# A two-layer graph network on one core: the order of work in the first hundred microseconds

## The chip, the cores and the metric

The kernel runs on one core of a Trainium2 chip, in one launch. The metric is the device time of that core in microseconds (us). Five instruction streams run side by side: TensorE (PE, with its weight loads PEld), VectorE (DVE), ScalarE (ACT), GpSimd (POOL) and SyncE (SP), which issues all the DMAs. Each stream executes its instructions in the order in which they were laid down[...].

## The reference

There are 64 graphs of 256 nodes with 512 features, and one adjacency matrix `adj` (256x256). Everything is float32.

```python
h = jnp.maximum(_layernorm(x, axis=-1), 0.0)
x = x + _L0_gnn_ref(h, adj, L0_gnn_W, L0_gnn_a)
h = jnp.maximum(_layernorm(x, axis=-1), 0.0)
x = x + _L1_gnn_ref(h, adj, L1_gnn_Wq, ...)
```

Layer 0 is a graph attention: `h = X @ W` (512 to 256 columns), two score columns `h @ a`, a leaky ReLU of their sum, the mask, a softmax, and `alpha @ h`; its result has 256 columns of `alpha @ h` and 256 of `h`. Layer 1 is an attention with 8 heads of 64: products of the normalized rows with Wq, Wk and Wv plus their biases, scores masked by `adj`, a softmax, the values weighed, and a product with Wo plus `bo`.

## The kernel before

**Groups and stages.** Two graphs form a group `g` of 512 rows (four tiles of 128), so there are 32 groups. `first_norm(g)` loads nothing itself: it measures the rows (`stats`), makes the normalized tiles `xn` on ACT, turns them, and puts them into `hT0`, the operand of layer 0. For group 0 the turning is done by transposes on PE (`pt`), for later groups by a round through memory: DVE transposes blocks into `xt`, SP sends `xt` to DRAM (`passed`) and fetches it back in another order (`moved`, four DMAs), and ACT copies it into the operand. `first_layer(g)` is layer 0: products `ph`, the tile `H`, the attention weights `e`, the products `po`, and then the second normalization into `hT1`, the operand of `project(g)`. `scores`, `weigh` and `outputs` are the attention and the last product (`sc`, `pr`, `py`).

For group 0 and 1, `first_layer` makes `ph` per row tile; the score row of group 1 goes from `H` by a DVE transpose (`rows`) to DRAM (`line`) and comes back spread over all partitions (`own`); then ACT makes `e` from it, DVE takes the leaky ReLU, ACT the exponential, and DVE multiplies it by `maskT`.

**Seven products.** The products with Wq, Wk, Wv, Wo and, from group 2 on, W are done by a scheme that multiplies two by two blocks with seven products in place of eight. Each product of `project` is four matmuls of 128x256. Products 1 and 2 use raw blocks of operand and weights. Product 6, 5, 7 and 3 need sums of operand blocks (`operand_sums`, four POOL instructions that write `sums` and a block of `hT`), and 3, 4, 5, 6, 7 need sums of weight blocks (`weight_sums`, four subtractions in place). Products 1, 6, 5 and 3 build up in one held bank of PSUM, and between them ACT takes copies (`kept`) out of it; 7 and 4 build up in a second one; product 2 uses one of the five turning banks of `mm`.

**The judge.** The kernel's fast path leaves out the subtraction of the row maximum. `judge()` shows that the inputs allow that: two products of each of Wq and Wk with itself (`gram`), squared twice (`square_q`, `square_k`, with ACT copies `room` between), and several sums of squares. `mask()` also tests that every row has an edge and that `adj` holds only 0 and 1 (`bad`).

**The bias of the values.** `last_bias()` multiplies the rows of Wo by `bv` (`bv_rows`, four DVE instructions), sums them on PE (`pb`) and adds the sum to `b_out`, which `residual` adds to `x` on POOL.

**The order.** The engines' order is written out by hand. `not_sooner` and `in_order` tie an instruction to the one issued last on its engine; all matmuls and transposes are in the order of the program. The prologue (lines 1135 to 1163) advances generators letter by letter: `n` is a piece of `first_norm`, `0` and `1` pieces of `first_layer` of groups 0 and 1, `u` a product of `project(0)`, `c` a piece of the judge, `e` a piece of the mask, `s` again a piece of group 1. From line 1165 the loop over groups does the same with the strings in `steps`. SP's stream holds, in this order: the first loads and weights, `passed` and `moved` for the first half of group 1, and then `late_loads` (line 235), which are the two loads of group 2, eight DMAs of Wo, eight of `bv` and one of `bo`; only behind these come `passed` and `moved` of the second half of group 1, then `line` and `own`.

The prologue's lines in the kernel before:

```python
take(*"en00nn0e00n0cnn")
late_loads()
take(*"000n0c00n0n")
weight_sums("q")
take(*"euun0011")
order = "- nss n nn ns - s - ss ss s s n - n - s - s".split()
```

Of the kernel before, what the change touches and what calls it, by code (L numbers as in the profile page):

```python
# [57 lines left out]
def bounded(  # L58
# [87 lines left out]

    def warm_up():
        warm = mm("warm")
        for _ in range(12):
            matmul(warm[:, :P], square_ones, square_ones, start=True, stop=True)  # L150

    def load(g, b):
# [35 lines left out]
    def mask():  # L188
        edge = att.tile([P, NT, N], F32, tag="kept", name="edge", bufs=3)
        not_sooner(vector, "tensor_scalar", edge, adj_i, 0.0, None, op0=ALU.not_equal)  # L190
        yield
        pt = mm("pt_mask").rearrange("p (k q) -> p k q", k=NT)
        for kb in range(NT):
            for t in range(NT):
                transpose(
                    pt[:, kb, t * P : (t + 1) * P], edge[:, t, kb * P : (kb + 1) * P], ident
                )
        not_sooner(vector, "tensor_copy", maskT, pt)
        yield

        not_sooner(vector, "reduce_max", bad[:, 0, :], edge, axis=AX.X)
        vector.tensor_scalar(bad[:, 0, :], bad[:, 0, :], 0.0, None, op0=ALU.is_equal)
        vector.tensor_tensor(edge, edge, adj_i, op=ALU.not_equal)
        vector.reduce_max(bad[:, 1, :], edge, axis=AX.X)
        yield


# [22 lines left out]
    for name, src in (("q", bq), ("k", bk)):  # L230
        bcol[name] = const.tile([P, HP], F32, name=f"b{name}_sb")
        nc.sync.dma_start(bcol[name], src.rearrange("(c p) -> p c", p=P))
    load_weights("v", wvT)

    def late_loads():
        load(2, 0)
        load(2, 1)
        rows = woT.rearrange("(q j h d) o -> j h d q o", j=QH, h=2, d=S)
        bv_rows = bv.rearrange("(q j h d) -> j h d q", j=QH, h=2, d=S)
# [5 lines left out]
        for j in range(QH):  # L245
            for half in range(2):
                not_sooner(
                    sync, "dma_start", bv_col[j * S : (j + 1) * S, half, :], bv_rows[j, half]
                )
        not_sooner(  # L250
            sync, "dma_start", b_out,
            bass.AP(tensor=bo.tensor, offset=bo.offset, ap=[[0, P], [1, D]]),
        )

    rexp = const.tile([P, NT], F32, name="rexp")
    gpsimd.memset(rexp, -0.5)
# [9 lines left out]
    def first_weight_sums():  # L266
# [6 lines left out]
        not_sooner(gpsimd, "tensor_sub", t2, w22, w12)  # L273
        not_sooner(gpsimd, "tensor_sub", t4, w21, t2)

    def last_bias():


        rows = big.tile([P, 2, D // 2], F32, tag="oT0", name="bv_rows", bufs=1)
        for q in range(NQ):  # L280
            for half in range(2):
                of, by = w_sb["o"][:, half, 2 * q : 2 * q + 2, :], bv_col[:, half, q : q + 1]
                if q == half == 0:
                    not_sooner(vector, "tensor_scalar", rows, of, by, None, op0=ALU.mult)
                else:
                    vector.scalar_tensor_tensor(rows, of, by, rows, op0=ALU.mult, op1=ALU.add)
        yield
        pb = mm("pb")
        matmul(pb, square_ones, rows.rearrange("p o n -> p (o n)"), start=True, stop=True)
        yield  # L290
        not_sooner(vector, "tensor_add", b_out, pb, b_out)
        yield
# [133 lines left out]
            vector.bn_stats(st, src[t])  # L426
        vector.bn_aggr(mv[:, t, :], st)

    put_last, norm_last, edge_last, sums_last = [], [], [], []

    def norm_T(src, mv, name, by_pe):

# [46 lines left out]
        def turn(b):  # L479
# [10 lines left out]
            for t in tiles:  # L490
                not_sooner(
                    vector, "transpose",
                    xt[:, :, :, t % NT, :], xn[t].rearrange("p (c j a) -> p j c a", j=J, a=S),
                )
            rows = passed[b], xt.rearrange("p j c t n -> p j (c t n)")
            if name[:2] == "0_" and name not in ("0_0", "0_1"):
                not_sooner(sync, "dma_start", *rows)
# [347 lines left out]

    def project(g):
        ops = operands.pop(g)
        for name in ("q", "k", "v"):
            shape = [P, NT, D] if name == "v" else [P, HP, N]
            turn[0] = 1 - turn[0]  # L850

            def blocks(bank):
                return bank.rearrange("p (o n) -> p o n", o=2)

            def product(out, i, start):
                a, w = ops[i][0], w_sb[name][:, :, ops[i][1], :]
                for o in range(2):
                    cols = slice(o * P, (o + 1) * P)
                    for c in range(2):
                        of, by = (a[:, c, cols], w[:, c, :]) if name == "v" else (w[:, c, cols], a[:, c, :])  # L860
                        matmul(
                            out[:, o, :], of, by, start=start and o == c == 0, stop=o == c == 1,
                            skip_group_check=True,
                        )

            def part(b, half):
                if (name, g, b) not in qkv:
                    qkv[name, g, b] = place(shape, f"{name}_{g}_{b}")
                to = qkv[name, g, b][0]
                if name == "v":  # L870
                    return to[:, :, half * D // 2 : (half + 1) * D // 2]
                return to[:, 2 * half : 2 * half + 2, :]

            def take(to, bank, half):

                behind = [scalar.last] if g == 0 and name != "v" else []
                if name == "v":
                    taken = [scalar.copy(to, bank)]
                else:
                    taken = [  # L880
                        scalar.activation(
                            to[:, o, :], bank[:, o, :], AF.Identity,
                            bias=bcol[name][:, 2 * half + o : 2 * half + o + 1], scale=1.0,
                        )
                        for o in range(2)
                    ]
                for last in behind:
                    for instruction in taken:
                        after(instruction, last)

            def kept(bank, half, i):
                s = att.tile([P, 2, N], F32, tag="kept", name=f"kept{i}_{name}_{g}", bufs=3)
                take(s, bank, half)
                return s

            first = blocks(held_bank(turn[0], f"p{name}1_{g}"))
            product(first, 1, True)
            p1 = kept(first, 0, 0)
            yield
            second = blocks(mm(f"p{name}2_{g}"))  # L900
            product(second, 2, True)
            vector.tensor_add(part(0, 0), second, p1)
            yield
            product(first, 6, False)
            p16 = kept(first, 0, 1)
            yield
            second = blocks(held_bank(1 - turn[0], f"p{name}7_{g}"))
            product(second, 7, True)
            p7 = kept(second, 1, 2)
            yield  # L910
            product(first, 5, False)
            vector.tensor_add(part(1, 1), first, p7)
            yield
            product(second, 4, False)
            vector.tensor_add(part(1, 0), second, p16)
            yield
            product(first, 3, False)
            take(part(0, 1), first, 1)
            yield

    def value_differences(g, b):

# [205 lines left out]
    def take(*names):  # L1128
        for name in names:
            next(work[name])  # L1130
# [461 lines left out]
```

## Time and profile before

| | us |
|---|---|
| median of 3 runs | 2413.16 (2413.15 to 2413.9) |
| the profiled execution: device time | 2416.09 |
| the profiled execution: span of the trace | 2414.4 |
| PE busy | 2387.8 |
| DVE busy | 1697.8 |
| POOL busy | 1422.3 |
| ACT busy | 1021.7 |

The profiled execution is 2.9 us longer than the median of the others, and 1.7 us of it lie outside its span. Matmul busy time covers 99% of the span, and the chain of work that ended last runs over PE for 96% of it. The 26.6 us in which no matmul ran lie almost wholly in the first 110 us and in the last 40. In lines of the timeline an entry gives start, duration, engine, source line, operation, output and inputs, and how often; a bracket gives idle time before it and what ended it. "SPq" lines are DMA issues on SP.

### The profile page before, as it was taken

What the parts mean: (1) busy time and instruction counts of PE and PEld (TensorE: products, weight loads), DVE (VectorE), ACT (ScalarE), POOL (GpSimd) and SP (SyncE); (2) the same over time, 40 slices, a digit from 0 to 9 for tenths busy, and PEclk for the clock granted to TensorE, in tenths of its full rate; (3) what the DMA queues carried; (4) which work ended last, traced back from release to release, by engine and by line L of the source; (5) the groups of instructions that cost most, each with busy time, mean ns of one, the idle gap of its engine ahead of it and who ended that gap; (6) DMA issues with size and microseconds to landing.
All of it is one profiled execution on the core that took longest, in us unless ns stands there. A gap on an engine that the chain in (4) does not pass through costs nothing.

```text
span 2414.4 us, 43064 instructions
## 1 busy us (share of the span) xinstructions
PE 2387.8 (99%) x15812; PEld 2012.6 (83%) x15812; DVE 1697.8 (70%) x3346; ACT 1021.7 (42%) x2017; POOL 1422.3 (59%) x1290
## 2 busy tenths in 40 slices
PE   7999999999999999999999999999999999999998
PEld 6788888888888888888888888888888888888886
DVE  6677767777667767667776667676677676676666
ACT  4444444444434444434444444444344344343431
POOL 3466666566566556565655666565655565656552
PEclk9999999999999999999999999999999999999999
DMA  5244444444455444544444544444554445554331
GB/s 179 92 142 143 139 155 149 144 153 139 142 159 160 144 136 140 157 148 154 152 136 139 161 149 145 145 143 145 153 166 145 136 136 162 149 159 141 111 103 44
DMA packets 272041, 343.76 MB, mean 142 GB/s; under 512 B 25424, under 2 KB 217168, under 8 KB 271824
## 3 DMA queue, kind: packets, MB, share of 16 engines
q1 hardware_dynamic: 271824, 340.95, 45.7%
q8 instruction: 126, 2.06, 0.4%
q14 instruction: 91, 0.75, 0.1%
HBM read 177.22 MB, written 163.64 MB: 141 GB/s over the span
## 4 chain that ended last, share of the span: by engine, by line
PE 96%; DVE 2%; DMA 1%; ACT 1%; issue 0%; SPq 0%; POOL 0%; DVEq 0%; ACTq 0%
PE pk L137 16%; PE py L137 16%; PE pv L137 16%; PE pq L137 16%; PE sc L137 10%; PE pr L137 9%; PE ph L137 8%; PE po L137 4%; DMA passed<-xt 0%; DVE st L35 0%; DVE x L35 0%; DMA wo_sb<-in_L_gnn_Wo_dram 0%; ACT e L35 0%; PE total L137 0%; DVE xt L35 0%
## 5 line engine op out<-in xcount | busy, mean ns | idle before, releaser
L35 POOL TENSOR_TENSOR p<-p 128x512 f32<-128x512 f32 x248 | 384.4, 1562 | 484.0 <-DVE p L35 466.6
L35 ACT ACTIVATE xn<-x,factor 128x512 f32<-128x512 f32 x256 | 194.8, 807 | 343.9 <-POOL factor L35 338.4
L35 DVE TENSOR_TENSOR p<-p,maskT 128x1024 f32<-128x1024 f32 x254 | 334.0, 1335 | 1.9 <-ACT p L35 1.9
L35 ACT ACTIVATE p<-sc 128x512 f32<-128x512 f32 x512 | 257.7, 624 | 138.0 <-PE sc L137 120.2
L35 DVE TENSOR_TENSOR x<-py,x 128x256 f32<-128x256 f32 x448 | 185.7, 415 | 184.4 <-PE py L137 178.1
L35 POOL TENSOR_TENSOR parts<-parts 128x512 f32<-128x512 f32 x248 | 248.1, 1000 | 83.5 <-DMA parts<-rows 61.2
L137 PE MATMUL py<-wo_sb,oT 128*128 128x256 f32 x1024 | 262.4, 379 | 0.6 <-DVE oT L35 0.6
L137 PE MATMUL sc<-q,k 64*128 64x256 f32 x2048 | 252.3, 390 | 0.3 <-ACT p L35 0.3
L137 PEld LDWEIGHTS sc<-q,k 64*128 64x128 f32 x2048 | 204.5, 186 | 48.6 <-issue 25.9
L137 PE MATMUL pk<-hT,wk_sb 128*128 128x256 f32 x1024 | 244.8, 382 | 0.0
L137 PE MATMUL pq<-hT,wq_sb 128*128 128x256 f32 x1024 | 240.1, 382 | 1.0 <-ACT hT L35 0.7
L137 PE MATMUL pv<-wv_sb,hT 128*128 128x256 f32 x1024 | 236.8, 379 | 0.0
L137 PE MATMUL pr<-p,v 128*32 128x256 f32 x4096 | 234.2, 380 | 0.0
L137 PEld LDWEIGHTS pq<-hT,wq_sb 128*128 128x128 f32 x1024 | 191.8, 190 | 36.7 <-issue 10.3
L35 POOL TENSOR_TENSOR factor<-factor,rexp 128x2 f32<-128x2 f32 (+1 forms) x132 | 116.6, 883 | 176.3 <-DVE factor L35 175.9
L137 PEld LDWEIGHTS py<-wo_sb,oT 128*128 128x128 f32 x1024 | 194.2, 190 | 28.2 <-DVE oT L35 1.1
L137 PEld LDWEIGHTS pk<-hT,wk_sb 128*128 128x128 f32 x1024 | 189.6, 190 | 33.2 <-issue 9.9
L137 PEld LDWEIGHTS pv<-wv_sb,hT 128*128 128x128 f32 x1024 | 194.5, 190 | 26.9 <-issue 0.5
L137 PEld LDWEIGHTS pr<-p,v 128*32 128x32 f32 x4096 | 126.8, 110 | 97.8 <-issue 15.3
L137 PE MATMUL py<-wo_sb,o_sums 128*128 128x256 f32 x768 | 197.6, 380 | 1.4 <-DVE x L35 1.3
L137 PE MATMUL pv<-wv_sb,sums 128*128 128x256 f32 x768 | 181.6, 379 | 1.8 <-ACT kept_v L35 1.8
L137 PE MATMUL pq<-sums,wq_sb 128*128 128x256 f32 x768 | 181.5, 379 | 1.3 <-POOL sums L35 1.3
(150 smaller groups left out, 4083.9 us busy)
## 6 DMA issues: line engine op xcount, KB each, us to landing
passed<-xt SPq DMA_DIRECT2D x124, 512.0 KB, 3.1
moved<-passed SPq DMA_DIRECT2D x496, 128.0 KB, 3.4
rows<-p SPq DMA_DIRECT2D x124, 512.0 KB, 3.4
parts<-rows SPq DMA_DIRECT2D x496, 128.0 KB, 3.0
x<-in_x_dram SPq DMA_DIRECT2D x64, 512.0 KB, 4.4
out_dram<-x SPq DMA_DIRECT2D x62, 512.0 KB, 4.0
own<-line SPq DMA_DIRECT2D x31, 256.0 KB, 3.1
wq_sb<-in_L_gnn_Wq_dram SPq DMA_DIRECT2D x2, 512.0 KB, 8.7
```

What stands on the lines that cost most here:

```text
L35: instruction = getattr(self.engine, operation)(*args, **kwargs)
L137: in_order(nc.tensor.matmul(*args, **kwargs))
```

## The change

SP: `bv` and `bo` are loaded straight behind the value weights; the loads of group 2 keep their place behind the first half of group 1; the eight DMAs of Wo go behind the second half of group 1.

PE: the seven products of a projection become a generator of their own, `projection`, and for group 0 they run in the order `qqkkqqqqqkkkkkvvvvvvv`, so that products 1 and 2 of k stand between products 2 and 6 of q. Product 1 of k takes the held bank 2 for that. The squares of the judge move from around the first products of k into the later products of q; `gram_k` moves behind the fourth `po` of group 0; `pb` moves behind one more value product; and 18 products of ones stand at the start in place of 12.

DVE: the mask's two tests move out of the weight sums of k to before and behind the copy of `maskT`; the transposes of group 1's first half move behind the first two tiles of group 0's `po`; the weight sums of k move behind a product of q; `bv_rows` moves behind the transposes of group 1's second normalization, tied by `turn_last`.

POOL: the sums of W move behind one more `factor`, and one piece of `residual`, the last, moves from the last group's first half to the end of the group ahead of it.

The diff, with the unchanged body of `projection` cut:

```diff
     def warm_up():
         warm = mm("warm")
-        for _ in range(12):
+        for _ in range(18):
...
     def mask():
...
+        not_sooner(vector, "reduce_max", bad[:, 0, :], edge, axis=AX.X)
+        not_sooner(
+            vector, "tensor_scalar", bad[:, 0, :], bad[:, 0, :], 0.0, None, op0=ALU.is_equal
+        )
         yield
...
-        not_sooner(vector, "reduce_max", bad[:, 0, :], edge, axis=AX.X)
-        vector.tensor_scalar(bad[:, 0, :], bad[:, 0, :], 0.0, None, op0=ALU.is_equal)
-        vector.tensor_tensor(edge, edge, adj_i, op=ALU.not_equal)
-        vector.reduce_max(bad[:, 1, :], edge, axis=AX.X)
+        not_sooner(vector, "tensor_tensor", edge, edge, adj_i, op=ALU.not_equal)
+        not_sooner(vector, "reduce_max", bad[:, 1, :], edge, axis=AX.X)
         yield
...
     load_weights("v", wvT)
+    bv_rows = bv.rearrange("(q j h d) -> j h d q", j=QH, h=2, d=S)
+    for j in range(QH):
+        for half in range(2):
+            nc.sync.dma_start(bv_col[j * S : (j + 1) * S, half, :], bv_rows[j, half])
+    nc.sync.dma_start(b_out, bass.AP(tensor=bo.tensor, offset=bo.offset, ap=[[0, P], [1, D]]))
 
     def late_loads():
-        load(2, 0)
-        load(2, 1)
         rows = woT.rearrange("(q j h d) o -> j h d q o", j=QH, h=2, d=S)
...
                 if q == half == 0:
-                    not_sooner(vector, "tensor_scalar", rows, of, by, None, op0=ALU.mult)
+                    made = vector.tensor_scalar(rows, of, by, None, op0=ALU.mult)
+                    for other in turn_last:
+                        after(made, other)
...
     def project(g):
         ops = operands.pop(g)
-        for name in ("q", "k", "v"):
...
+        parts = {name: projection(g, name, ops) for name in "qkv"}
+        for name in "qqkkqqqqqkkkkkvvvvvvv" if g == 0 else "q" * 7 + "k" * 7 + "v" * 7:
+            next(parts[name])
+            yield
+
+    def projection(g, name, ops):
+        shape = [P, NT, D] if name == "v" else [P, HP, N]
+        turn[0] = 1 - turn[0]
+        firsts = 2 if (g, name) == (0, "k") else turn[0]
+        sevenths = 1 - turn[0]
...
-    take(*"en00nn0e00n0cnn")
+    take(*"en00nn0e00ne0cn000n")
+    load(2, 0)
+    load(2, 1)
+    take(*"n00c0n0n")
     late_loads()
-    take(*"000n0c00n0n")
     weight_sums("q")
-    take(*"euun0011")
-    order = "- nss n nn ns - s - ss ss s s n - n - s - s".split()
-    for i, parts in enumerate(order, 2):
+    take(*"uunuu0011")
+    order = "- - nss n nn ns s ss ss s s n - n s - s".split()
+    for i, parts in enumerate(order, 4):
         next(products)
-        if i == 13:
+        if i in (4, 6):
+            take(*"cc")
+        if i == 4:
+            take("c")
+        if i == 17:
             weight_sums("o", gpsimd)
-        if i == 5:
+        if i == 10:
             first_weight_sums()
-        if i in (2, 7):
-            weight_sums("kv"[i // 7])
+        if i in (6, 10):
+            weight_sums("kv"[i // 10])
+        if i == 12 and NG > 3:
+            load(3, 0)
+            load(3, 1)
...
-        if i in (6, 8):
-            take(*"cc")
-        if i == 7:
-            take("c")
-        if i == 8 and NG > 3:
-            load(3, 0)
-            load(3, 1)
-        if i in (12, 18, 19):
+        if i in (16, 19, 20):
             next(bias)
...
             elif g == NG - 1:
-                parts = ("Smmoomoomooor", "Smmoomoomooo")[b]
+                parts = "Smmoomoomooo"
+            elif (g, b) == (NG - 2, 1):
+                parts += "r"
```

More of the change, by code (lines that the diff above doesn't have):

```diff
@@ L233, in bounded @@
     load_weights("v", wvT)
+    bv_rows = bv.rearrange("(q j h d) -> j h d q", j=QH, h=2, d=S)
[3 more added lines that the diff above has]
+    nc.sync.dma_start(b_out, bass.AP(tensor=bo.tensor, offset=bo.offset, ap=[[0, P], [1, D]]))
     def late_loads():
-        load(2, 0)
-        load(2, 1)
         rows = woT.rearrange("(q j h d) o -> j h d q o", j=QH, h=2, d=S)
-        bv_rows = bv.rearrange("(q j h d) -> j h d q", j=QH, h=2, d=S)
         for j in range(QH):
@@ L244, in late_loads @@
                 )
[L245 to L253, printed above, removed]
     rexp = const.tile([P, NT], F32, name="rexp")
@@ L274, in first_weight_sums @@
         not_sooner(gpsimd, "tensor_sub", t4, w21, t2)
+    put_last, norm_last, edge_last, sums_last, turn_last = [], [], [], [], []
     def last_bias():
@@ L427, in stats @@
         vector.bn_aggr(mv[:, t, :], st)
-    put_last, norm_last, edge_last, sums_last = [], [], [], []
     def norm_T(src, mv, name, by_pe):
@@ L494, in turn @@
                 )
+            turn_last[:] = [vector.last]
             rows = passed[b], xt.rearrange("p j c t n -> p j (c t n)")
@@ L847, in project @@
         ops = operands.pop(g)
-        for name in ("q", "k", "v"):
[L849 to L898, printed above, removed]
-            yield
[L900 to L919, printed above, removed]
@@ new lines, in project, with blocks, product, part @@
+        parts = {name: projection(g, name, ops) for name in "qkv"}
+        for name in "qqkkqqqqqkkkkkvvvvvvv" if g == 0 else "q" * 7 + "k" * 7 + "v" * 7:
+            next(parts[name])
+            yield
+    def projection(g, name, ops):
[3 more added lines that the diff above has]
+        sevenths = 1 - turn[0]
+        def blocks(bank):
+            return bank.rearrange("p (o n) -> p o n", o=2)
+        def product(out, i, start):
+            a, w = ops[i][0], w_sb[name][:, :, ops[i][1], :]
+            for o in range(2):
+                cols = slice(o * P, (o + 1) * P)
+                for c in range(2):
+                    of, by = (a[:, c, cols], w[:, c, :]) if name == "v" else (w[:, c, cols], a[:, c, :])
+                    matmul(
+                        out[:, o, :], of, by, start=start and o == c == 0, stop=o == c == 1,
+                        skip_group_check=True,
+                    )
+        def part(b, half):
+            if (name, g, b) not in qkv:
+                qkv[name, g, b] = place(shape, f"{name}_{g}_{b}")
+            to = qkv[name, g, b][0]
+            if name == "v":
+                return to[:, :, half * D // 2 : (half + 1) * D // 2]
+            return to[:, 2 * half : 2 * half + 2, :]
+        def take(to, bank, half):
+            behind = [scalar.last] if g == 0 and name != "v" else []
+            if name == "v":
+                taken = [scalar.copy(to, bank)]
+            else:
+                taken = [
+                    scalar.activation(
+                        to[:, o, :], bank[:, o, :], AF.Identity,
+                        bias=bcol[name][:, 2 * half + o : 2 * half + o + 1], scale=1.0,
+                    )
+                    for o in range(2)
+                ]
+            for last in behind:
+                for instruction in taken:
+                    after(instruction, last)
+        def kept(bank, half, i):
+            s = att.tile([P, 2, N], F32, tag="kept", name=f"kept{i}_{name}_{g}", bufs=3)
+            take(s, bank, half)
+            return s
+        first = blocks(held_bank(firsts, f"p{name}1_{g}"))
+        product(first, 1, True)
+        p1 = kept(first, 0, 0)
+        yield
+        second = blocks(mm(f"p{name}2_{g}"))
+        product(second, 2, True)
+        vector.tensor_add(part(0, 0), second, p1)
+        yield
+        product(first, 6, False)
+        p16 = kept(first, 0, 1)
+        yield
+        second = blocks(held_bank(sevenths, f"p{name}7_{g}"))
+        product(second, 7, True)
+        p7 = kept(second, 1, 2)
+        yield
+        product(first, 5, False)
+        vector.tensor_add(part(1, 1), first, p7)
+        yield
+        product(second, 4, False)
+        vector.tensor_add(part(1, 0), second, p16)
+        yield
+        product(first, 3, False)
+        take(part(0, 1), first, 1)
+        yield
```

## The prediction

> **What bounds the kernel now.** The page gives PE 2387.8 of 2414.4 us, and the chain that ended last is PE to 96%, so time can be won only where no matmul runs, or where one runs slowly. I read the view of who waited for whom first, for PE (total, times, longest), then PE's timeline for the places:
>
> ```profile
> PE ph L137 <- ACT hT L35: 8.4, 2, 7.8
> PE pt L140 <- ACT xn L35: 2.6, 3, 1.3
> PE square_q L137 <- ACT room L35: 2.3, 1, 2.3
> PE pv L137 <- ACT kept_v L35: 1.8, 2, 1.2
> PE py L137 <- DVE x L35: 1.3, 3, 0.9
> PE pq L137 <- POOL sums L35: 1.3, 1, 1.3
> ...
> PE pq L137 <- ACT hT L35: 0.7, 1, 0.7
> ```
>
> All but `py` lie ahead of 107 us. From 30 us to there the waits are 0.68, 0.98, 0.57, 1.28, 7.80, 2.35, 0.57 and 1.25, in sum 15.48. The largest is explained by SP's timeline:
>
> ```profile
> 32.77 8.98 SPq L35 DMA_DIRECT2D wo_sb<-in_L_gnn_Wo_dram  x8
> 41.79 3.71 SPq L35 DMA_DIRECT2D bv_col<-in_L_gnn_bv_dram  x8
> 45.55 0.43 SPq L35 DMA_DIRECT2D b_out<-in_L_gnn_bo_dram  x1
> 46.07 0.38 SPq L35 DMA_DIRECT2D passed<-xt  x1
> 51.50 1.75 SPq L35 DMA_DIRECT2D moved<-passed  x4
> ```
>
> DVE had the second half's `xt` at 37.96 (transposes from 36.67, 1.29), but SP was busy with the loads and issued `passed` only at 46.07; it landed after 5.4 us where the first half's took 3.0. PE then starts `ph` like this:
>
> ```profile
> 47.14 1.89 PE L137 MATMUL pq<-hT,wq_sb 128*128 128x256 f32 x8
> 56.83 6.79 PE L137 MATMUL ph<-w_sb,hT 128*128 128x258 f32 x16 [7.80 <-ACT hT L35]
> 63.45 1.89 PE L137 MATMUL pq<-sums,wq_sb 128*128 128x256 f32 x8
> ```
>
> The 16 matmuls take 6.6 us to the next start; the first such 16 took 3.5 (the chain has them at 17.06). The view by stretches (PE busy, granted clock, DMA share, GB/s) shows why:
>
> ```profile
> 4.99:8.40 3.41, 1.75 (x14) 1.00 1.03 258
> 8.40:11.81 3.41, 3.41 (x11) 0.50 1.02 367
> ...
> 42.53:45.94 3.41, 2.13 (x10) 1.00 0.19 35
> ...
> 59.60:63.00 3.40, 3.40 (x9) 0.50 0.00 0
> 73.25:76.67 3.42, 1.07 (x6) 1.00 0.96 302
> 76.67:80.08 3.41, 3.41 (x17) 0.50 0.36 132
> ```
>
> After a stretch of 3.41 us busy to 51% or less the next runs at half clock; at 62% it doesn't. That adds 3.1 us behind the long wait, and at 76.38 `square_q`, `square_k` and the next product take 5.26 where 0.89+0.89+1.73 = 3.51 is usual, 1.75 more.
>
> [...]POOL's `sums` took 1.66 to 1.73 beside DVE's weight sums, 1.27 alone. [...]`passed` (512 KB) took 3.02 on an idle queue.
>
> **The change part by part.** I laid out the changed order engine by engine, each instruction starting when its engine and its inputs are free, with the durations of before: a product 1.73 (63.45 to 65.18), a `ph` tile 1.75, a `po` 0.87, a square 0.89; on ACT a pair of `kept` 0.74, `xn` 0.71, a copy of `moved` 0.52, four `e` 1.6, an exponential 0.63; on DVE 0.61 for 128x512 with two inputs, 1.83 for a `po` tile with its statistics; `passed` 3.05, `moved` 4.7 with its four issues, `line` 1.75, `own` 3.1. The same laying for the order of before gives 16.65 us of waits against 15.48 measured, 8.38 for the 7.80 and 2.17 for the 2.35, so it is good to about a tenth.
>
> *Start.* 24 warm matmuls run cold, 0.2 us each, until 4.99, and end at 5.9; the window to 8.40 is 51% busy and the first `ph` runs cold, 5.0 us for 16. Twelve more at 0.11 end at 7.0 to 7.3, about when `pt` is released (7.24); the window becomes some 80% busy and `ph` takes 3.5. Then the two score columns wait for DVE, which ends at 13.67; they start at 13.7 in place of 14.72. Gain 1.0. The phase of the window differs from run to run: if the clock comes late, the twelve cost up to 0.5; if early, the gain reaches 1.7.
>
> *Mask tests.* The 2.3 us on DVE now stand in its idle times of 3.08 ahead of `maskT` (0.9) and 2.13 ahead of `e` (1.4 of 2.13): nothing lost. *SP and gram_k.* The nine issues of `bv` and `bo` (4.1 us) stand where SP is idle until 26.9. `passed` of the first half starts at 29.6 instead of 26.9, since its transposes stand behind two `po` tiles (2 x 1.83 less the 1.0 won); its copies are still in time at 38.2, ACT being busy until then. With `po` ahead of `gram_k`, PE has no wait there.
>
> *k's first two products* (3.46 us, bank 2 is free) fill PE from 36.1 to 39.5: the waits of 0.98 and 0.57 go; 0.85 ahead of the first product of q stays. POOL starts `sums` at 41.3 with DVE idle, 1.29 each, and the second is ready at 43.9, when `ph` ends: the 1.28 goes.
>
> *The second half of group 1.* `xt` ends at 36.6, `passed` lands at 40.3 (I allow 0.6 for the load of group 2 beside it), `moved` at 45.0. Wo's issues follow at 42.0 to 51.0, clear of `line` at 58. PE reaches `ph` at 52.7 now, behind the four squares. But ACT's two squares stand ahead of its copy of `moved`: 0.2 from the end of the last square, 0.70 for ACT's, 0.62 for the copy: a new wait of 1.56. The squares' own wait of 2.35 goes, products 7 and 5 of q lie between.
>
> *What is late next.* Behind `ph` PE has only five products (8.65 us) ahead of group 1's `po`; before it had 19.9 us, with the mask product ready at 78.9 and `po` at 83.36. The chain from `ph`'s end, 57.8: copy, `rows`, `line`, `own` to 63.5; ACT has the two `xn` of group 2 and a pair of `kept_k` to 65.4 first; `e` and the leaky ReLU on DVE to 67.7; then DVE has three weight sums of v (2.05), the sum of k (0.62), the fourth weight sum (0.61), and the mask (0.73): 71.75. PE waits 0.82 for that `kept_k` and is done at 67.26: 4.49 us of new wait. This is long enough for half clock: the window in which PE resumes and perhaps the next. Cold for 1.7 to 5.3 us costs 0.9 to 2.7; I take 2.0.
>
> *Values.* With `bv_rows` behind the transposes, `kept_v` of product 6 is not late and the 1.25 goes; the first 0.57 stays (0.58). *Scores.* ACT now copies v and then all four halves of `hT` ahead of the exponentials, so these start 2.8 us behind the first score instead of 1.6 (109.03 less 107.40), and the third pair of scores waits for a bank: 1.24.
>
> *End.* POOL's last `residual` runs beside DVE's mask products at 2374.16 and stretches them to 1.82 and 1.62 where the last graph has 1.21; `py` waits 0.87 and 0.21 there, 0.26 for the last graph. Gain 0.8. POOL is idle where it goes.
>
> Sum: the waits fall from 15.48 to 0.85+1.56+0.82+4.49+0.58+1.24 = 9.54, so 5.9; half clock from 4.85 to 2.0, so 2.85; start 1.0; end 0.8: 10.6 us. The profiled execution would go from 2416.09 to 2405.5, and the median, which is 2.9 lower, from 2413.16 to 2402.6. The difference of the two I carry along unexplained.
>
> **Rivals.** A measurement of this kernel can tell about 0.2% (4.8 us) from no change.
> - The new wait is larger (13%): POOL's four sums of W (3.2 us) lie beside DVE's part of that chain and could hold it up by most of their length, to a wait of 7.5 and two cold windows, 3.4: 3.0+1.4 lost, and the 1.56 wait, alone in one window (54% busy, between the 51 and 62 seen), 1.7 more in some cases: 2407 to 2408.7, I take 2407.5. For it: DVE took 1.42 for each later `bv_rows` beside POOL. Against it: half of that chain is DMA and ACT.
> - The new wait is small (12%): with `own` early and DVE not held up, under 2 us and no cold window, 2.5+2.0 more: 2398. Against it: the order of DVE is fixed, 3.3 us stand ahead of the mask.
> - The DMA round is what counts, not its place (4%): `passed` again slow, `moved` late by more than the 8 us it now has to spare; the long wait stays in part: 2410.
> - Slower (4%): ACT enters the loop 1.2 us later against PE, and each half of a group passes that on as a wait of `sc` for `p`. The price is 62 halves times the wait, and from 0.17 us each it eats the gain; at 0.4 it is 24.8 - 10.6, so 2427. Against it: from 130 to 2370 us PE waited only 0.3 in all, ACT is 42% busy and takes up such a lag.
>
> **How the numbers follow.** 67% for the forecast, 2402.6, with 2399.5 to 2406.5 as its own range: the new wait between 3 and 6, its cold time 0.9 to 2.7, the start -0.5 to 1.7. The range to 8 in 10 reaches to both first rivals: 2398.5 to 2408. Faster by over 0.2% means below 2408.3: the forecast, the small wait and most of the larger one, 0.87; within, 0.09; slower 0.04.
>
> **What would show it.** Right: `passed` of the second half issued below 40 us and no wait of `ph` over 2 us; `ph` at full clock at 9 us; a wait of `po` for `e` of 3 to 6 us near 68 with half clock behind it; `sc` waiting about 1 us for `p`; the scores beginning near 96.4 (107.4 less 7.2 of waits ahead of them, 2.85 and 1.0). Wrong: waits of `sc` in the loop, or the half clock elsewhere.

## The result, and the profile after

| | before | changed |
|---|---|---|
| median | 2413.15 us (2411.73 to 2413.9, 8 runs) | 2405.68 us (2404.38 to 2406.9, 8 runs) |
| profiled execution | 2416.09 us, span 2414.4 | 2405.35 us, span 2403.7 |

The ratio is 0.997, with a 95% interval of 0.9959 to 0.9981: 7.5 us less by the medians, 10.7 by the two profiled executions. The view of who waited for whom, for PE, changed kernel (total, times, longest):

```profile
PE po L137 <- DVE e L35: 5.3, 1, 5.3
PE sc L137 <- ACT p L35: 1.6, 2, 1.3
PE ph L137 <- ACT hT L35: 1.3, 1, 1.3
...
PE pk L137 <- ACT kept_k L35: 0.8, 1, 0.8
...
PE pv L137 <- ACT kept_v L35: 0.6, 1, 0.6
...
```

The wait of `ph` for `hT` is down from 7.80 us to 1.34, and that of 2.35 for `room` is gone; a wait of 5.28 for the mask product has come, and one of `sc` for `p`. SP's timeline shows the second half's round through memory:

```profile
37.19 0.34 SPq L35 DMA_DIRECT2D passed<-xt  x1
41.97 1.75 SPq L35 DMA_DIRECT2D moved<-passed  x4
...
```

`passed` goes out at 37.19 instead of 46.07. It took 4.8 us to the issue of `moved`, more than the 3.6 that I had allowed with 0.6 for the load of group 2, but ACT is not ready to copy `moved` before 54.07, so this costs nothing. PE's timeline at the places that the prediction names:

```profile
9.10 3.70 PE L137 MATMUL ph<-w_sb,hT 128*128 128x256 f32 x16
...
36.05 3.62 PE L137 MATMUL pk<-hT,wk_sb 128*128 128x256 f32 x16
...
54.73 3.75 PE L137 MATMUL ph<-w_sb,hT 128*128 128x258 f32 x16 [1.34 <-ACT hT L35]
...
73.42 3.76 PE L137 MATMUL po<-H,e 128*128 128x257 f32 x8 [5.28 <-DVE e L35]
76.98 2.96 PE L137 MATMUL pk<-hT,wk_sb 128*128 128x256 f32 x8
...
97.15 2.42 PE L137 MATMUL sc<-q,k 64*128 64x256 f32 x18
100.87 2.10 PE L137 MATMUL sc<-q,k 64*128 64x256 f32 x14 [1.30 <-ACT p L35]
```

The first `ph` runs at full clock (16 matmuls in 3.70 us, 5.01 in the profile of before), k's first products fill the gap at 36, and the scores begin at 97.15 instead of 107.40. Behind the 5.28 the two `po` take 3.56 us to the next start (in a version without the half clock, further down, 1.81) and the product 2.79 (usually 1.73). By stretches (PE busy first, after the five engines the granted clock):

```profile
65.47:68.88 3.41, 1.99 (x8) 1.44 (x8) 2.60 (x4) 2.85 (x7) 3.15 (x5) 1.00 0.59 166
68.88:72.30 3.42, 0.00 (x0) 0.00 (x0) 3.35 (x5) 1.36 (x3) 0.59 (x1) 1.00 0.85 294
72.30:75.71 3.41, 2.29 (x6) 1.86 (x7) 1.75 (x4) 0.00 (x0) 0.00 (x0) 0.50 0.00 0
75.71:79.12 3.41, 3.41 (x10) 2.69 (x9) 3.05 (x9) 0.00 (x0) 0.00 (x0) 0.50 0.00 0
```

Behind one window (a stretch of 3.41 us) without a matmul the next two ran at half clock (0.50), which cost 2.8 us by those starts. What fills PE's gap is in the second line: DVE is busy 3.35 of 3.42. DVE's timeline:

```profile
66.93 1.95 DVE L35 SCALAR_TENSOR_TENSOR e<-e 128x512 f32<-128x512 f32 x2 [0.81 <-ACT e L35]
68.80 2.67 DVE L35 TENSOR_TENSOR wv_sb<-wv_sb 128x512 f32<-128x512 f32 x3
71.39 0.69 DVE L35 TENSOR_TENSOR k<-pk,kept_k 128x512 f32<-128x512 f32 x1
71.99 0.68 DVE L35 TENSOR_TENSOR wv_sb<-wv_sb 128x512 f32<-128x512 f32 x1
72.59 1.29 DVE L35 TENSOR_TENSOR e<-e,maskT 128x512 f32<-128x512 f32 x2
```

From the end of the leaky ReLU near 68.9 to the mask at 72.59 DVE does four weight sums of v and the sum of k, none of which PE needs yet.

### The profile page after: what moved, and what is told of

Its sections match the earlier page's. It is cut to its first block, busy times and chain, and to the rows that moved or that the text cites. A ratio compares the mean times of both kernels' runs of the same rounds, so it can differ in the third digit from the quotient of the medians.

```text
span 2403.7 us, 43081 instructions
## 1 busy us (share of the span) xinstructions
PE 2384.2 (99%) x15824; PEld 2011.0 (84%) x15824; DVE 1692.1 (70%) x3346; ACT 1021.8 (43%) x2017; POOL 1421.4 (59%) x1290
## 4 chain that ended last, share of the span: by engine, by line
PE 97%; DVE 1%; ACT 1%; DMA 1%; issue 0%; POOL 0%; SPq 0%; ACTq 0%; DVEq 0%
PE py L137 16%; PE pq L137 16%; PE pk L137 16%; PE pv L137 16%; PE sc L137 10%; PE pr L137 9%; PE ph L137 8%; PE po L137 5%; DVE st L35 0%; DMA passed<-xt 0%; ACT hT L35 0%; DVE x L35 0%; DMA moved<-passed 0%; PE total L137 0%; DMA x<-in_x_dram 0%
## 5 line engine op out<-in xcount | busy, mean ns | idle before, releaser
L35 DVE TENSOR_TENSOR p<-p,maskT 128x1024 f32<-128x1024 f32 x254 | 327.7, 1311 | 3.9 <-ACT p L35 3.9
L137 PE MATMUL pk<-sums,wk_sb 128*128 128x256 f32 x768 | 181.6, 379 | 0.8 <-ACT kept_k L35 0.8
```

The costliest lines, as they stand in the source:

```text
L35: instruction = getattr(self.engine, operation)(*args, **kwargs)
L137: in_order(nc.tensor.matmul(*args, **kwargs))
```

## The experiments

Each was timed beside the kernel before, unchanged, on the same chip; its median there was 2411.3 us for the first four, 2411.82 for the next four, 2411.78 for two and 2411.43 for the last two. The changed kernel has its own time only in the result above, where the kernel before had 2413.15, so a row is best compared with it by the ratio (0.997, 0.9959 to 0.9981); a difference of medians can be off by 1 to 2 us. The first question is what the gain is owed to (SP's order, the order of PE, or the clock at the start), the second what the new waits come from.

| kernel | median us | ratio to before, 95% |
|---|---|---|
| the kernel before, again | 2412.13 | 1.0004 (0.9996 to 1.0012) |
| before, only SP's loads moved | 2404.69 | 0.9974 (0.9964 to 0.9985) |
| changed, 12 products of ones | 2404.89 | 0.9974 (0.9964 to 0.9985) |
| changed, Wo's loads early again | 2404.96 | 0.9975 (0.9965 to 0.9985) |
| changed, v's weight sums early | 2401.67 | 0.9958 (0.9945 to 0.9972) |
| the same, second squares late | 2399.65 | 0.9951 (0.9938 to 0.9965) |
| the same, first `hT` before v | 2399.25 | 0.9949 (0.9935 to 0.9962) |
| changed, last `residual` as before | 2407.24 | 0.998 (0.9972 to 0.9988) |
| changed, W's sums later | 2403.88 | 0.9969 (0.9958 to 0.998) |
| all of these improvements | 2397.63 | 0.9942 (0.9929 to 0.9956) |
| changed, SP as before | 2408.6 | 0.9992 (0.9983 to 1.0) |
| before, SP's loads and last `residual` moved | 2402.33 | 0.9966 (0.9952 to 0.9979) |

**The kernel before, again.** No edit. It asks what the 2.9 us are by which the profiled execution of before exceeded the median. (The 1.7 us between device time and span are no part of them: in every run the device time is 1.6 to 1.8 us above the span.)

> The kernel before, run again unchanged, to learn why the profiled pair differs by 10.7 us and the medians by 7.5. Theory 1: the first profiled execution of before was one whose clock windows fell badly (17.1 us of half clock in three stretches); other executions keep full clock in one or two of these places. Then the time is 2413 (2411.5 to 2414), the granted clock is above 0.996 in most executions, and the profile has less than 17.1 us of half clock, with the same waits of PE. Theory 2: the 2.9 us are a cost of that profile spread over the span; then the profile of this run shows the same three half-clock stretches and its span is again near 2411.5 without any difference in waits or clock.

PE's and SP's timelines of this execution:

```profile
54.11 6.59 PE L137 MATMUL ph<-w_sb,hT 128*128 128x258 f32 x16 [4.94 <-ACT hT L35]
```

```profile
32.89 6.03 SPq L35 DMA_DIRECT2D wo_sb<-in_L_gnn_Wo_dram  x8
...
44.29 0.38 SPq L35 DMA_DIRECT2D passed<-xt  x1
48.85 1.75 SPq L35 DMA_DIRECT2D moved<-passed  x4
```

The same eight issues of Wo took 6.03 us here and 8.98 in the first profile; `passed` took 4.5 instead of 5.4. The long wait is 4.94 instead of 7.80, 2.86 less, and the span is 3.4 shorter (2411.0); 2.9 of the 3.4 are there when the scores begin (104.48 instead of 107.40). Neither theory holds as it was put: half clock is less, 13.7 us instead of 17.1, but in the same three places, and the waits are not the same. So the size of the wait that the change removes is a sample of something that varies, and the first profile had the larger one of the two. Why SP's issues took longer in one execution was not traced.

**SP alone.** Only the loads on SP are moved: Wo, `bv` and `bo` all go behind the second half of group 1, where the change puts `bv` and `bo` at the front. PE, DVE, ACT and POOL keep the order of before.

```diff
     def late_loads():
-        load(2, 0)
-        load(2, 1)
...
     take(*"en00nn0e00n0cnn")
-    late_loads()
+    load(2, 0)
+    load(2, 1)
     take(*"000n0c00n0n")
+    late_loads()
```

> Of the whole change only the place on SP's queue: the loads of group 2 stay, the loads of Wo, bv and bo go behind the second half of group 1. Theory 1 (the queue's place is the largest term): the wait of ph falls from 7.8 to about 1.7 and no half clock follows it, the other waits of before stay: 2413.2 - 6.1 - 3.1 = 2404, as fast as the whole change within 2 us. Theory 2 (it is the filling of PE with k's first products and the moved squares that gives the gain): 2410 or more.

PE's timeline:

```profile
50.53 3.75 PE L137 MATMUL ph<-w_sb,hT 128*128 128x258 f32 x16 [1.44 <-ACT hT L35]
...
67.04 1.16 PE L137 MATMUL square_q<-room 128*128 128x128 f32 x8 [2.34 <-ACT room L35]
...
72.39 1.90 PE L137 MATMUL po<-H,e 128*128 128x257 f32 x8
```

2404.69 us: this move alone reaches the ratio of the whole change within the noise (0.9974 and 0.997; the intervals overlap). The wait of `ph` is 1.44, and there is no half clock behind it (3.75 us for the 16 matmuls); the squares still wait 2.34, but `po` waits for nothing, since eleven products and squares stand between it and `ph`.

**The 18 products of ones** back to 12, in the changed kernel.

```diff
-        for _ in range(18):
+        for _ in range(12):
```

> The changed kernel with 12 products of ones at the start in place of 18. Theory 1: the first ph runs at half clock in the profile and 1 us is lost, 2406.7 (2405.7 to 2407.4, by the window's phase). Theory 2: the start is hidden behind the waits that follow or the phase decides it alone: 2405.7 within 0.3.

2404.89, no loss. The clock came up later in this execution: its 24 matmuls of ones ended at 6.41 us, and at 5.90 in the first profile of before, where the clock came at 4.99. PE's timeline:

```profile
8.73 3.70 PE L137 MATMUL ph<-w_sb,hT 128*128 128x256 f32 x16
```

`ph` is at full clock with 12 too. By an estimate from those two ends (in the profile of before a matmul of ones starts every 0.21 us ahead of the clock and every 0.11 behind it) the clock came at 6.1, and the window from there was 66% busy. In the first profile of before the clock came at 4.99, that window was 51% busy, and the clock fell again for the one to 11.81. The version with all improvements, further down, has 18 products, and its clock came at 4.99 too:

```profile
4.99:8.40 3.41, 2.89 (x24) 2.48 (x23) 2.36 (x9) 2.45 (x3) 1.59 (x6) 1.00 1.04 266
```

That window is 85% busy, with 24 matmuls in place of 14, and `ph` ran at full clock. The other profiles agree: of the five executions with 12 products three, in which the ones ended at 5.86 to 6.04, ran `ph` partly at half clock (4.86 to 5.19 us); in two, where they ended at 6.41 and 6.49, it ran at full clock (3.70, and 13 of its 16 matmuls in 3.05). With 18 it took 3.70 to 3.72 in seven profiles, among them the changed kernel's, with the clock at 4.03, and the one above. So the traces show the six more products at work where the clock comes early. In the median nothing of it can be seen.

**Wo early again, PE as changed.**

```diff
+    late_loads()
     take(*"n00c0n0n")
-    late_loads()
     weight_sums("q")
```

> The changed kernel with the eight loads of Wo ahead of the second half of group 1 again, all else changed. Theory 1 (the two large parts fill the same hole): passed is issued near 45 instead of 37.2, moved lands near 55.7, and since PE has k's first products and the squares to do until 53.4 the wait of ph grows only from 1.3 to about 3, with or without a half-clock window behind it: 2407.4 to 2409. Theory 2 (the parts add): the whole wait of 7.8 and its half clock come back: 2414 or more.

2404.96 us, nothing lost. SP's timeline and PE's:

```profile
36.39 4.72 SPq L35 DMA_DIRECT2D wo_sb<-in_L_gnn_Wo_dram  x8
41.50 0.35 SPq L35 DMA_DIRECT2D passed<-xt  x1
46.58 1.73 SPq L35 DMA_DIRECT2D moved<-passed  x4
```

`passed` is 4.3 us later than in the changed kernel, took 5.1, and `moved` still lands ahead of the end of ACT's squares (ACT copies it at 53.99, with no wait for it); `ph` waits 1.34 as there. With bv and bo out of the way, PE's new order covers Wo's place. It left open whether that order would have been enough with the whole of the old queue.

**SP as before, all else as changed**: bv and bo too go back between the load of group 2 and the second half.

```diff
-    bv_rows = bv.rearrange("(q j h d) -> j h d q", j=QH, h=2, d=S)
-    for j in range(QH):
-        for half in range(2):
-            nc.sync.dma_start(bv_col[j * S : (j + 1) * S, half, :], bv_rows[j, half])
...
+                not_sooner(
+                    sync, "dma_start", bv_col[j * S : (j + 1) * S, half, :], bv_rows[j, half]
+                )
...
+    late_loads()
     take(*"n00c0n0n")
-    late_loads()
```

> Edit: all loads of SP in the order of the kernel before (Wo, bv and bo between the load of group 2 and passed of the second half); PE, DVE, ACT and POOL as changed. Theory 1 (PE's order alone covers the late passed): passed goes out near 45 us, moved lands near 54, just when ACT has done its squares, so ph waits 1.3 to 3 us and the time stays within 1.5 us of the changed kernel, about 2405. Theory 2 (bv and bo are what counts; 4 us more in the queue bring the long wait back): ph waits 4 us or more, with half clock behind it, 2409 or above.

2408.6 us, and a ratio that hardly differs from 1. PE's timeline:

```profile
56.94 5.44 PE L137 MATMUL ph<-w_sb,hT 128*128 128x258 f32 x16 [3.57 <-ACT hT L35]
```

`passed` goes out at 47.34, and ACT waits for `moved` until 56.27. The wait is 3.57, between what the two theories had, and cold time follows: 16 matmuls take 5.28 to the next start instead of 3.59. This is near theory 2: of the 5.8 us by which `passed` is later than in the run before, the nine issues of bv and bo are 4.5. All the rest of the change together, without SP's part, is worth 2.8 us by the medians, 1.9 by the ratio, 0 to 4 by its interval.

**v's weight sums early** takes the surplus of the new wait away.

```diff
-        if i in (6, 10):
-            weight_sums("kv"[i // 10])
+        if i == 6:
+            weight_sums("k")
+            weight_sums("v")
```

> Edit: v's four weight sums on DVE go into its idle time ahead of `rows` (beside k's), out of the gap between `e` and the mask product. Theory 1 (the new wait of po for the mask is DVE's order: 2.67+0.69+0.68 us stand between the leaky ReLU and the mask): the wait of 5.28 us falls to about 1.2 (0.69 for the sum of k may stay), and as PE stays busy in that window the half clock of 6.83 us behind it goes too (2.9 us by the durations of po and pk): together 6 to 7 us, so about 2398 where the changed kernel has 2405. Theory 2 (the chain over own and ACT's e decides): the wait stays above 4 us and the half clock with it, time within 1 us of the changed kernel. Theory 3 (the wait goes, the half clock comes elsewhere): about 4 us.

PE's timeline:

```profile
70.70 1.97 PE L137 MATMUL po<-H,e 128*128 128x257 f32 x8 [2.02 <-DVE e L35]
```

The wait of `po` fell from 5.28 to 2.02, not to the 1.2 expected, and the half clock behind it went (1.81 and 1.73 us to the next starts, where the changed kernel has 3.56 and 2.79); `pv` now waits 1.21 for `kept_v` instead of 0.61. The scores begin at 92.21, 4.9 us earlier. Of that 2.9 (by the ratios) to 4.0 (by the medians) reached the time, and the two intervals overlap. By stretches, further on:

```profile
93.17:96.58 3.41, 1.60 (x14) 1.09 (x12) 0.00 (x0) 2.59 (x6) 0.60 (x1) 1.00 0.80 264
96.58:99.99 3.41, 3.41 (x14) 2.34 (x14) 3.08 (x2) 2.96 (x6) 3.33 (x3) 0.50 0.80 197
```

`sc` now waits 1.81 us for `p`, the window around it is 47% busy, and the next is at half clock, which by my estimate costs 1.7 us (half of 3.41). So theory 1 is right on the cause of the wait, and theory 3 on the clock in this execution and on the time.

**The second squares late** as well: ACT's squares no longer stand ahead of its copy of `moved`.

```diff
-        if i in (4, 6):
+        if i == 4:
             take(*"cc")
...
+        if i == 6:
+            take(*"cc")
```

> Edit: v's weight sums as in the run before it in this call, and the judge's second squares go behind the ph of group 1, so that ACT copies moved first. Theory 1 (ph waits because ACT's two squares stand ahead of its copy): the wait of ph of 1.3 us goes, about 1.3 us better than with the sums alone, 2397. Rival (DMA decides: moved has only just landed): the wait of ph stays, no gain; or the squares now wait themselves (square_q for room, up to 2.3 us as in the kernel before) and take it back.

PE's timeline:

```profile
52.19 3.65 PE L137 MATMUL ph<-w_sb,hT 128*128 128x258 f32 x16
```

The wait of `ph` is gone and the squares don't wait either; the scores begin at 90.85, 1.4 us earlier. The median fell by 2.0 us, to 2399.65, and the mean granted clock of this execution is 1.000. This is theory 1; some of the 2.0 can be the cold window at 96.58, which this execution doesn't have.

**The first `hT` copies ahead of v's**, on ACT.

```diff
-            behind = [scalar.last] if g == 0 and name != "v" else []
+            behind = [scalar.last] if g == 0 and (name != "v" or ends) else []
...
-        take(part(0, 1), first, 1)
+        take(part(0, 1), first, 1, True)
```

> Edit: the two above, and ACT's copies of the first hT halves of group 1's layer 1 go ahead of v's copy at the end of group 0's projection, so that the exponentials follow sooner. Theory 1 (sc waits for p because ACT copies v and four hT ahead of the exponentials): the wait of sc of 1.3 us falls below 0.4, 1 us better again, 2396. Rival: the wait only moves to another product (weigh for v, or pq for hT), no gain.

ACT's timeline:

```profile
87.53 1.14 ACT L35 COPY hT<-moved 128x512 f32<-128x512 f32 x2 [2.71 <-PE pv L137]
90.11 0.59 ACT L35 COPY v<-pv 128x512 f32<-128x512 f32 x1 [1.45 <-PE pv L137]
92.18 1.14 ACT L35 COPY hT<-moved 128x512 f32<-128x512 f32 x2 [1.48 <-DMA moved<-passed]
93.22 4.00 ACT L35 ACTIVATE p<-sc 128x512 f32<-128x512 f32 x8
```

The order came out as meant, but `sc` still waits 1.44 and the time is the same. The second pair of `hT` copies stands ahead of the exponentials and waits 1.48 for its DMA. My theory was not enough: with ACT's copying out of the way the DMA of `moved` holds `sc` just as long. Putting that pair behind the exponentials wasn't tried.

**The end as before.**

```diff
-                parts = "Smmoomoomooo"
-            elif (g, b) == (NG - 2, 1):
-                parts += "r"
+                parts = ("Smmoomoomooor", "Smmoomoomooo")[b]
```

> Edit: the last piece of residual back in the last group's first half, as before the change; all else as changed. Theory 1 (POOL's residual beside DVE's mask products stretches them): the waits of py for x go back from 0.5 to about 1.3 us, time 0.8 us longer than the changed kernel, 2406. Rival (the end is not held up by it, the waits come from elsewhere): waits and time as in the changed kernel.

DVE's timeline, two mask products of the last group:

```profile
2367.77 1.83 DVE L35 TENSOR_TENSOR p<-p,maskT 128x1024 f32<-128x1024 f32 x1
2370.18 1.62 DVE L35 TENSOR_TENSOR p<-p,maskT 128x1024 f32<-128x1024 f32 x1
```

In the changed kernel both take 1.22. The waits of `py` are back at 1.3, 0.8 more, as forecast. The median is 1.6 us above the 2405.68 of the changed kernel; the intervals of the two ratios overlap, so the size of the rest isn't settled by this run. The next one looks at the same edit from the other side.

**Two edits in the kernel before**: SP's move alone, as above, and this last piece of `residual`; all else as before.

```diff
-                parts = ("Smmoomoomooor", "Smmoomoomooo")[b]
+                parts = "Smmoomoomooo"
+            elif (g, b) == (NG - 2, 1):
+                parts += "r"
```

> Edit: the kernel before with two parts of the change alone, SP's loads moved and the last piece of residual put at the end of the group ahead. If the gains add: waits of py for x from 1.3 to 0.5, time 0.8 to 1.6 us below SP's move alone, 2403 to 2404 and a ratio of 0.997, as good as the whole change or better. Rival: the end gives nothing measurable here, ratio 0.9974 as with SP's move alone.

PE's waits:

```profile
PE py L137 <- DVE x L35: 0.5, 2, 0.3
```

`py` waits 0.5 as in the changed kernel, and the time is 2402.33, 2.4 us below SP's move alone by the medians, of which 0.8 is the wait. In this execution the first `ph` ran at full clock, where it took 4.86 in the profile of SP's move alone (3.70 at full clock): some 1.2 more. So that the gains add is plausible, and the exact size is open, since the intervals overlap. What it does show is that these two edits are as good as the whole change, within the noise (0.9966 and 0.997).

**W's sums on POOL three products later**, so that they don't lie beside DVE's chain.

```diff
-        if i == 10:
+        if i == 13:
             first_weight_sums()
```

> Edit: the four subtractions of W on POOL go three products later, out of DVE's chain from `e` to the mask; all else as changed. Theory 1 (POOL stretches DVE's two-input instructions there: the leaky ReLU pair takes 1.95 us where the kernel before has 1.43 to 1.50, three weight sums 2.67 where it has 2.13): the pair comes down to about 1.45, the three sums to about 2.15, and the wait of po for the mask falls from 5.28 to about 4.3 us, near the 4.49 forecast; time about 1 us lower, 2404. Rival (the lengths are the instructions' own in this order, POOL has no part): durations and wait unchanged.

DVE's timeline:

```profile
67.26 1.49 DVE L35 SCALAR_TENSOR_TENSOR e<-e 128x512 f32<-128x512 f32 x2 [0.81 <-ACT e L35]
68.66 2.14 DVE L35 TENSOR_TENSOR wv_sb<-wv_sb 128x512 f32<-128x512 f32 x3
```

1.95 and 2.67 became 1.49 and 2.14, so 1.0 us, and the wait of `po` is 4.28 instead of 5.28. Nothing else of that chain changed: theory 1, and the missing 0.8 between forecast and measurement is POOL's. The half clock behind it cost 1.7 us by the starts (2.96 and 2.26, where 1.81 and 1.73 are usual), by my estimate one window. In the time the gain doesn't show (0.9969 and 0.997).

**All of it together**, W's sums later on top of the version with the early copies of `hT`.

> Edit: the same on top of the version with v's weight sums early, the second squares late and the early copies of hT. Theory 1: the leaky ReLU pair and the mask pair come down to about 1.45 and 1.25 us, the wait of po from 2.02 to about 1.2, time about 0.8 us lower than that version, 2398.4. Rival (what is won turns into a longer wait of sc for p, whose second copies of hT wait for moved): po's wait falls, sc's rises above 1.44 by as much, time unchanged at 2399.2.

PE's waits:

```profile
PE sc L137 <- ACT p L35: 1.4, 2, 1.1
PE pv L137 <- ACT kept_v L35: 1.3, 1, 1.3
...
PE po L137 <- DVE e L35: 1.0, 1, 1.0
```

2397.63 us, the lowest of all, 14 us below the kernel before and 7 to 8 below the changed one: ratio 0.9942 (0.9929 to 0.9956), the only one whose interval lies wholly below that of the changed kernel. `po` waits 1.02, and `sc` 1.14, less and not more, so the rival falls: the second copies of `hT` begin 1.1 us earlier too (91.09).

## Why the prediction was right, and where it was off

The forecast was 2402.6 us, the measurement 2405.68, inside the forecast's own range. The mechanism was the one described, with one reservation on the size of the gain, below. The terms of the sum, for the profiled pair:

| term | forecast | measured |
|---|---|---|
| waits, 15.48 before | 9.54 | 10.35 (0.72+0.34+1.34+0.76+5.28+0.61+1.30) |
| half clock, 4.85 before | 2.0 | 2.8 |
| start | 1.0 | 1.2 (14.72 to 13.51) |
| end | 0.8 | 0.8 |
| sum | 10.6 | 9.2, of 10.7 in all |

The 1.5 us that the sum leaves lie in small pieces. By the starts of the same matmuls the changed kernel is 8.8 us ahead where the scores end (102.90 and 111.72), 10.2 at PE's last product, and 10.7 at the end of the span: 0.4 of the rest lie ahead of the loop, 0.5 between there and PE's last product, 0.6 behind it. So 10.6 for the profiled pair was in part luck.

*The size of the long wait is why the median came out 3.1 us higher.* The term that was off is "The difference of the two I carry along unexplained". The 7.80 was taken as the kernel's own, while it was that execution's: 4.94 in another, with the span 3.4 shorter. With 4.94 in its place the same sum gives 10.6 less 2.86, so 7.7, and 2405.4 for the median; the medians show 7.5.

*The new wait* was seen at its place, with its cause and its order; 4.49 was 0.8 short. The forecast gave POOL's stretching of DVE to a rival with a price of 3 us. It did take place, and cost 1.0: the leaky ReLU pair took 1.95 us beside POOL's sums of W and 1.49 without them.

*The half clock* was 0.8 longer: two windows were cold, the "perhaps the next" of the forecast. The longer wait is not what decides this. Five executions here have the same wait of 5.28, and by the starts of `po` and `pk` it cost 2.8 us of half clock in the changed kernel, 2.7, 2.3 and 2.2 in the versions with the old end, with 12 products and with Wo early, and 1.8 with SP as before. What differed was how long the half clock went on after PE had resumed (5.7 us in the changed kernel, 3.7 by an estimate with SP as before, last section); the 2.0 was right within that.

*What the gain is owed to.* The forecast said nothing on this, but its terms do. Apart from SP's move, the start and the end, it had 0.98, 0.57, 1.28, 2.35 and 1.25 won, 6.43, with 1.75 of half clock, and 0.82, 4.49 and 1.24 to pay, 6.55, with 2.0: nothing in all. The runs agree: SP's move alone gives the measured gain within the noise, and the rest without it 2.8 us, where start and end had 1.8. The new waits (5.28, 0.76, 1.30 and 2.8 of half clock) eat what PE's new order wins. In the profiles SP's move alone has even ended its first scores at 100.74, 2.2 us ahead of the changed kernel, though its first `ph` ran cold.

*The start* gained 1.2, and the traces show the cause that was forecast, the 18 products, where the clock comes early; a gain in the median is not shown. *The scores' wait* had the forecast size (1.24 and 1.30) and, but for 0.31, the forecast cause. ACT's timeline, changed kernel:

```profile
97.74 1.14 ACT L35 COPY hT<-moved 128x512 f32<-128x512 f32 x2
99.18 1.14 ACT L35 COPY hT<-moved 128x512 f32<-128x512 f32 x2 [0.31 <-DMA moved<-passed]
100.23 1.08 ACT L35 ACTIVATE p<-sc 128x512 f32<-128x512 f32 x2
```

The exponentials start 3.1 us behind the first score, behind the copies of v and `hT` as forecast; what the forecast didn't have is that the DMA of the second pair is hardly earlier, and so holds `sc` once the copies come earlier. *The slower rival*, waits of `sc` in the loop, didn't come: between 110 and 2300 us PE waits 0.3 us for `kept_q` and 0.3 for `p`, no more.

## What to carry to other kernels

Before a gain is summed up, look at a second execution of the kernel before: a wait behind a row of DMA issues can differ between two executions (7.80 and 4.94 us here). When several edits attack the same hole, test each alone: here a moved block of DMA issues would have done, and the new order of PE's products added nothing measurable to it. And when PE is filled in one place, look at once for the consumer whose other engine is now too slow: moving four DVE instructions into DVE's own idle time took 3.3 us from the wait of `po` and 2.9 to 4.0 us from the time, with intervals that just overlap.

## What the runs showed of the hardware

*The granted clock.* In the first profiles of the two kernels it changed only at times that lie whole multiples of 3.41 us apart (before: 4.99, 8.40, 11.81, 52.77, 63.01, 76.67, 80.08 and 2411.38; changed: 72.30, 79.13 and 2403.60). The windows here are counted from such changes. Those in which matmuls took 0, 31, 47 and 51% were followed by half clock; with 55 (2396.78 in the changed kernel), 58 (65.47 there) and 62% not. The windows of 50 and 88% below don't fit a limit in between. Two windows of the version with two edits, then two of the version with the old end:

```profile
64.25:67.66 3.41, 1.69 (x15) 1.69 (x16) 3.34 (x6) 2.59 (x6) 0.00 (x0) 1.00 0.88 306
67.66:71.08 3.42, 3.42 (x19) 3.05 (x18) 0.84 (x2) 1.78 (x6) 0.00 (x0) 1.00 0.00 0
```

```profile
12.83:16.25 3.42, 3.00 (x28) 2.91 (x27) 3.04 (x11) 1.82 (x4) 0.63 (x1) 1.00 1.05 407
16.25:19.66 3.41, 3.41 (x10) 2.67 (x9) 3.20 (x9) 0.00 (x0) 0.72 (x1) 0.50 1.11 351
```

With 50% the clock stayed, and with 88% it fell; sixteen of the 28 matmuls of that window have two columns only. So the share of matmul time in the profile alone does not tell these windows apart; what does, no run here shows.

At half clock, a window 67% busy (2.29 at 72.30 above), and in the first profile of before one 81% busy (56.18 to 59.60: PE resumed at 56.83), was followed by another at half. A full one was followed by full clock in the seven cases that were measured: three in the first profile of before (8.40, 59.60, 76.67), two in its second one (56.49, 73.56), one in the changed kernel (75.71) and one with v's weight sums early (96.58). The same wait of 5.28 cost most (2.8 us) in the changed kernel, where PE resumed at 73.42 and the clock stayed at half until 79.13, 5.7 us more, and least (1.8) with SP as before, where by my estimate from the starts (twice the 1.84 lost) it stayed at half for 3.7.

*DMA issues and transfers.* The same eight issues of Wo took SP 3.7 to 9.0 us in different executions and places. The 512 KB of `passed` for the second half took 2.64 us from issue to the issue of `moved` in the profile of SP's move alone, where SP had issued nothing for 5 us ahead of it, and 4.5 to 5.4 in seven others, where other loads were issued within 1.3 us ahead of it. That those loads are the reason is likely, but not tested on its own.
